# Later loads of token tiles and packed weights, and a lower transfer rate in the plan, in a transformer layer on one core

## The chip, the cores and the metric

The kernel runs on one core of a Trainium2 chip. The metric is device time in microseconds, the median of several executions; smaller is better. The core has five instruction streams that matter here: PE (matrix products; PEld is its loading of weights), DVE, ACT and POOL (elementwise work), and SP, which here only issues DMA transfers. Each stream runs its instructions strictly in the order in which the program lists them and waits wherever an operand isn't ready.

## The reference

One layer with layer norms ahead of its two halves: attention with 32 heads of 32 columns, one shared key and value head, a linear position bias and a causal mask; then one linear map whose weight is packed in six-bit codes. The input is 4 batches of 512 tokens of 1024 columns.

```
q = (LN(x) @ Wq).reshape(b, s, 32, 32)
k, v = split(LN(x) @ Wkv)                       # one head of 32 for all 32 query heads
scores = q k^T / sqrt(32) + slope[h] * (kpos - qpos), masked where kpos > qpos
x = x + (softmax(scores) @ v) @ Wo
codes = 4 six-bit numbers out of each 3 words of qweight     # 1024 x 768 int32 -> 1024 x 1024
x = x + LN(x) @ ((codes - zero_point) * weight_scale)^T + bias
```

## The kernel before

**Work.** Products with Wq and Wo are made of three products each, a high part and a low part of both operands (`hi`, `lo`), to keep precision. The kernel goes through the 4 batches; each batch of 512 tokens has 4 token tiles of 128 (`x_b_t`, loaded by `load_x`, L550), which `layernorm` (L563) normalizes and `chunk` (L591) transposes on PE into eight tiles `xc`. Then come 8 steps for each batch, one for every group of 4 heads, 32 steps in all:

- `queries` (L675): 24 products into the one buffer `pq`; ACT and DVE copy it out as `qh` and `ql` (one buffer each); both are written to DRAM (`q_d`) and read back in another layout as `qs` (three loads) beside the bias rows (`qr_d`).
- `maxima` (L726): products `s` of queries and keys; DVE takes row maxima of them (L751, `junk`); PE turns the maxima (`trm`), and they go as two rows `mt` into `qs` by two small DMAs.
- `attention` (L797): products `st` with those rows in place, exponentials on ACT (`p`), masking and sums of `p` on POOL, products `pav` with the values, and the sums `den`.

After the steps come 16 token tiles (`token_tile`, L995): product with Wo (`po`), layer norm, transposes, product with the unpacked codes (`pf`), and the store.

**Packed weights.** `unpack` (L904) handles an eighth of `qweight`: a load of 393 KB (`qw`, L908), three DVE instructions (`v`), an ACT conversion (`code`), a transposing DMA (`across`, L942), a second ACT conversion (`codes`, L945), and a write of 524 KB to DRAM (`wf_d`). The result is read back only once, by `load_codes` (L952), after the attention steps.

**What sets the order.** The program's order is made on the host by the class `Work`. Every operation is entered with an engine, a cost and a wished time `at` in microseconds. `forward` (L248) runs a model of the five streams: an operation may start when those ahead of it have ended, and not before its `hold`; among the ready ones the earliest wished goes first. In the model a transfer takes `size / DMA_RATE` on one shared DMA resource (L265), plus a fixed latency; with 280.0 that is 1.87 us for 524e3 bytes. `backward` (L285) finds how late each could be, and `order` (L311) repeats both and keeps the order whose modelled end is earliest. In the later passes a transfer is also kept from starting more than `EARLY`, 12 us, ahead of its latest useful time. Before the change only transfers that POOL issues have a `hold`. The model becomes the order in which the instructions stand on each engine; it puts no waiting on the chip beyond the real operands.

**Buffers that matter.** `xc` has 10 tiles: a batch's eight `xc`, and two that `unpack` uses in turn for `qw`, `v` and `codes`. `x` has 4 tiles. `qs` has 3.

The lines at the end of the kernel that set the wished times are these (STEP is 15.0, T0 is 16.0, NG is 8):

```
    for c in range(KC):
        unpack(T0 + (1.6 + 2.0 * (c % 3) + NG * (c // 3)) * STEP, c)
...
        if b:
            for t in range(NT):
                load_x(T - 3.0 * STEP + 3.0 * t, b, t)
            for t in range(NT):
                layernorm(T - 2.0 * STEP + 3.0 * t, b, t)
```

Of the kernel before, what the change touches and what calls it, by code (L numbers as in the profile page):

```python
# [118 lines left out]
class Work:  # L119
# [6 lines left out]
    DMA_LAT = 2000  # L126
    EARLY = 12e3
    TURN = 105
    DMA_RATE = 280.0

    def __init__(self):
        self.ops, self.items = [], []
# [115 lines left out]
    def forward(self, wanted, hold=None):  # L248
# [13 lines left out]
        def done(o, s):  # L262
            if o.size:
                free = s + self.ISSUE[o.eng]
                shared["dma"] = max(shared["dma"], free) + o.size / self.DMA_RATE  # L265
                seen[o.n] = shared["dma"] + self.DMA_LAT
# [18 lines left out]
    def backward(self, start):  # L285
# [7 lines left out]
        def first(o):  # L293
            away = o.size / self.DMA_RATE + self.DMA_LAT if o.size else 0.0
            t = away
            for m in self.edges[o.n]:
                if not o.size:
                    away = self.SAME[o.eng] if self.ops[m].eng == o.eng else o.lat
                t = max(t, until[m] + away)
            return t  # L300
# [36 lines left out]
STEP = 15.0  # L337
# [4 lines left out]
def layer_kernel(  # L342
# [14 lines left out]
    nc = tc.nc  # L357
# [3 lines left out]
    NG = NH // GH  # L361
# [4 lines left out]
    work = Work()  # L366
# [14 lines left out]
    def new(pool_name, tag, shape, dt, name):  # L381

        p, bufs = pools[pool_name]
        return work.item(lambda: p.tile(shape, dt, tag=tag, name=name), (pool_name + tag, bufs))
# [13 lines left out]
    def act(at, n, fn, out, ins, sbuf=False):  # L398
        work.op("ACT", at, n / 1.2 + (90.0 if sbuf else 70.0), fn, out, ins)

    def dve(at, n, fn, out, ins, port=False, more=0.0):
        work.op("DVE", at, n / 0.96 + 75.0 + more, fn, out, ins, port=port)
# [1 line left out]
    def pool_op(at, cost, fn, out, ins):  # L404
        work.op("POOL", at, cost, fn, out, ins, port=True)

    def dma(at, size, fn, out, ins, eng="SP"):
        work.op(eng, at, 0.0, fn, out, ins, size=size)

    def split(at, n, hi, lo, src, hi_it, lo_it, src_it, port=False):  # L410

# [7 lines left out]
    def move(dst, src):  # L419
        return nc.sync.dma_start(out=dst.bitcast(F32), in_=src.bitcast(F32))  # L420
# [22 lines left out]
        out=mask(),  # L443
        in_=mask(),
# [14 lines left out]
    def prep_keys(at, i):  # L459
        dma(  # L460
            at, 61e3, lambda: nc.gpsimd.dma_start(out=kst[i]()[R_BIAS:R_ALL, :], in_=k_rows),
            [(kst[i], "b")], [], eng="POOL",
        )

    def prep_rows(at, g):
        dma(
            at, 229e3, lambda: nc.gpsimd.dma_start(out=qr_d[g], in_=q_rows[g]), [qr_i[g]], [],
            eng="POOL",
        )
# [4 lines left out]
    def prep_wkv(at):  # L474
        st = new("stg", "stg", [P, KC, 2 * HD], F32, "wkv_st")
        src = w_kv.rearrange("(c p) d -> p c d", p=P)
        dma(at, 262e3, lambda: nc.sync.dma_start(out=st(), in_=src), [st], [])
        split(
            at + 18.0, HALF, lambda: wkv()[:, :, 0 : 2 * HD], lambda: wkv()[:, :, 2 * HD :], st,
            (wkv, 0), (wkv, 1), st, port=True,  # L480
        )
# [68 lines left out]
    def load_x(at, b, t):  # L550
        xt = xh[b, t] = new("x", "x", [P, H], F32, f"x_{b}_{t}")
        src = x[b, ts(t, P), :]
        if b or t < NT - 1:
            dma(at, 524e3, lambda: nc.sync.dma_start(out=xt(), in_=src), [xt], [])
            return
        for i in range(2):
            dma(
                at + 0.001 * i, 262e3,
                lambda i=i: nc.sync.dma_start(out=xt()[:, ts(i, HALF)], in_=src[:, ts(i, HALF)]),
                [(xt, i)], [],  # L560
            )
# [342 lines left out]
    def unpack(at, c):  # L904

        qw = new("xc", "xc", [P, H // 4, 3], I32, f"qw_{c}")
        src = qweight[ts(c, P), :].rearrange("p (g w) -> p g w", w=3)
        dma(at, 393e3, lambda: nc.sync.dma_start(out=qw(), in_=src), [qw], [])  # L908
        v = new("xc", "xc", [P, H // 4, 4], I32, f"v_{c}")
        dve(  # L910
            at + 4.0, 256,
            lambda: nc.vector.tensor_scalar(
                v()[:, :, 0:1], qw()[:, :, 0:1], 63, None, ALU.bitwise_and
            ),
            [(v, 0)], [qw], port=True,
        )
        dve(
            at + 4.0, 256,
            lambda: nc.vector.tensor_scalar(
                v()[:, :, 1:2], qw()[:, :, 0:1], 6, 63, ALU.logical_shift_right, ALU.bitwise_and  # L920
            ),
            [(v, 1)], [qw], port=True,
        )
        dve(
            at + 4.0, 256,
            lambda: nc.vector.tensor_scalar(
                v()[:, :, 2:4], qw()[:, :, 1:3], 63, None, ALU.bitwise_and
            ),
            [(v, 2)], [qw], port=True,
        )  # L930
        code = new("stg", "stg", [P, H], BF16, f"code_{c}")
        act(
            at + 5.0, H,
            lambda: nc.scalar.activation(
                code(), v().rearrange("p g j -> p (g j)"), AF.Copy, bias=-CODE_MID
            ),
            [code], [v], sbuf=True,
        )
        across = new("stg", "stg", [P, KC, P], BF16, f"across_{c}")
        dma(  # L940
            at + 6.0, 700e3,
            lambda: nc.sync.dma_start_transpose(out=across(), in_=code()), [across], [code],  # L942
        )
        turned = new("xc", "xc", [P, KC, P], F32R, f"codes_{c}")
        act(at + 12.0, H, lambda: nc.scalar.copy(turned(), across()), [turned], [across], sbuf=True)  # L945
        dma(
            at + 14.0, 600e3,
            lambda: move(wf_d.rearrange("k p n -> p k n")[:, :, ts(c, P)], turned()),
            [(wf_i, c)], [turned],
        )  # L950
# [266 lines left out]
    T0 = 16.0  # L1217
    for t in range(NT):
        load_x(0.01 * t, 0, t)
        layernorm(1.0 + t, 0, t)  # L1220
# [4 lines left out]
        prep_wq(2.0 if g == 0 else T0 + (g - 0.9) * STEP, g)  # L1225
        prep_rows(T0 + g * STEP + (2.0 if g == 0 else -6.0), g)
    for c in range(KC):
        unpack(T0 + (1.6 + 2.0 * (c % 3) + NG * (c // 3)) * STEP, c)
    for b in range(B):
        T = T0 + b * NG * STEP  # L1230
        if b:
# [5 lines that stand above are left out]
            chunk(  # L1237
                T - 4.0 + 0.5 * c if b == 0 else T - 0.9 * STEP + 1.3 * c - 2.6, b, c
            )
        keys_values(T + 6.0 if b == 0 else T - 1.0, b)  # L1240
        for g in range(NG):
            i = b * NG + g
            at = T0 + i * STEP
            queries(at, i)
            maxima(at + 17.0, i)
            attention(at + 34.0, i)
        invert(T + NG * STEP + 48.0, b)
# [52 lines left out]
```

## Time and profile before

| | us |
|---|---|
| median of 3 runs | 826.74 (825.87 to 827.88) |
| the profiled execution | 825.42 |
| its span, first to last instruction | 823.5 |
| PE busy | 795.9 |
| DVE busy | 565.5 |
| POOL busy | 514.1 |
| ACT busy | 372.3 |

The span lies 1.9 us under the profiled execution's time, and that execution 1.3 us under the median. A busy PE is not a PE at its peak: matmuls overlap, and a matmul that is shown with 390 ns is followed by the next after 227 ns where nothing disturbs it. So the busy share of PE says little, and the stretches in which it waits, or in which its clock is low, say more. "PEclk" in the profile is the clock that was granted, as a share of the full one. "DMA share" is the mean busy share of the 16 DMA engines; it passes 1 in places. An entry "[1.45 <-DVE ql L415]" behind an instruction says that its engine stood idle for 1.45 us before it, and that this DVE instruction ended the wait.

### The profile page before, as it was taken

How to read it: one execution, taken by the hardware profiler on the slowest of the kernel's cores; microseconds unless marked ns; L12 is line 12 of the kernel's file. 1: busy time of each engine (PE TensorE's matmuls, PEld its weight loads, DVE VectorE, ACT ScalarE, POOL GpSimd, SP SyncE). 2: the span in 40 equal slices, each digit the busy share in tenths (PEclk: the TensorE clock that was granted, in tenths of full speed). 3: DMA queues.
4: the chain of work that ended last, by engine and by line, in shares of the span. 5: the costliest groups of instructions: out<-in, count | busy, mean ns of one | idle time of the engine just before them, and what ended most of it. 6: DMA issues, size and time to landing. Idle time of an engine off the chain costs nothing.

```text
span 823.5 us, 13425 instructions
## 1 busy us (share of the span) xinstructions
PE 795.9 (97%) x4480; PEld 594.7 (72%) x4480; DVE 565.5 (69%) x1491; ACT 372.3 (45%) x659; POOL 514.1 (62%) x442
## 2 busy tenths in 40 slices
PE   5979999999999999999999999999999999999997
PEld 4756676777676767676775767667888888888885
DVE  7476777388786388777367675644998666666865
ACT  4336575464775445675556564330233323332320
POOL 4337977276787375877489896879465445554333
PEclk9989999999999999999999999999999999999999
DMA  7885853395553387543567966526875755665321
GB/s 223 245 252 154 232 164 91 111 266 188 155 145 100 106 262 211 148 120 111 174 174 194 235 189 208 170 58 171 214 178 158 173 131 129 152 151 137 97 52 51
DMA packets 131796, 133.39 MB, mean 162 GB/s; under 512 B 42964, under 2 KB 93140, under 8 KB 130704
## 3 DMA queue, kind: packets, MB, share of 16 engines
q1 hardware_dynamic: 130912, 129.01, 57.0%
q0 software_dynamic: 816, 3.53, 1.7%
q8 instruction: 35, 0.57, 0.3%
q14 instruction: 33, 0.27, 0.1%
HBM read 85.58 MB, written 39.85 MB: 152 GB/s over the span
## 4 chain that ended last, share of the span: by engine, by line
PE 89%; DVE 4%; DMA 2%; ACT 2%; issue 1%; POOL 1%; SPq 1%; DVEq 0%; ACTq 0%; POOLq 0%
PE po L1047 21%; PE pq L682 21%; PE pf L1167 13%; PE st L819 9%; PE s L738 9%; PE pav L848 8%; PE den L877 4%; PE pkv L616 2%; PE tr L598 2%; DVE junk L751 2%; ACT p L829 1%; POOL p L860 1%; DMA wo_st<-in_L_attn_Wo_dram 1%; DMA qs<-mt 1%; SPq L420 1%
## 5 line engine op out<-in xcount | busy, mean ns | idle before, releaser
L751 DVE CUSTOM_DVE_ANT_0 junk<-s,mask 128x384 f32<-128x384 f32 (+3 forms) x512 | 250.6, 490 | 119.6 <-PE s L738 88.8
L860 POOL TENSOR_TENSOR p<-p,p 128x1536 f32<-128x1536 f32 (+2 forms) x96 | 232.4, 2421 | 16.7 <-PE pav L848 15.0
L829 ACT ACTIVATE p<-st 128x512 f32<-128x512 f32 (+1 forms) x352 | 183.9, 559 | 115.8 <-PE st L819 110.7
L682 PE MATMUL pq<-xc,wqh 128*128 128x512 f32 x512 | 198.5, 405 | 2.3 <-DVE ql L415 1.4
L1047 PE MATMUL po<-woh,aT 128*128 128x512 f32 x512 | 164.8, 391 | 0.0
L838 POOL TENSOR_SCALAR_AFFINE_SELECT p<-p 128x512 f32<-128x512 f32 x128 | 82.2, 647 | 105.1 <-ACT p L829 104.3
L738 PE MATMUL s<-kst,qs 124*128 124x384 f32 (+3 forms) x512 | 127.5, 324 | 3.9 <-DVE mx L751 3.6
L819 PE MATMUL st<-qs,kst 126*128 126x512 f32 (+1 forms) x352 | 127.1, 399 | 3.9 <-ACT p L829 2.9
L1167 PE MATMUL pf<-wf,xT 128*128 128x512 f32 x512 | 121.1, 390 | 0.7 <-DVE xT L415 0.7
L738 PEld LDWEIGHTS s<-kst,qs 124*128 124x128 f32 x512 | 91.5, 189 | 34.2 <-DVE mx L751 8.9
L682 PEld LDWEIGHTS pq<-xc,wqh 128*128 128x128 f32 x512 | 97.7, 191 | 23.8 <-issue 2.7
L1047 PEld LDWEIGHTS po<-woh,aT 128*128 128x128 f32 x512 | 96.1, 188 | 21.7 <-DVE mx L751 0.8
L1167 PEld LDWEIGHTS pf<-wf,xT 128*128 128x128 f32 x512 | 95.8, 188 | 20.9 <-DVE xT L415 1.1
L682 PE MATMUL pq<-xc,wql 128*128 128x512 f32 x256 | 101.8, 398 | 0.1
L1047 PE MATMUL po<-wol,aT 128*128 128x512 f32 x256 | 99.7, 389 | 0.0
L819 PEld LDWEIGHTS st<-qs,kst 126*128 126x128 f32 x352 | 63.5, 190 | 25.7 <-ACT p L829 10.8
L848 PE MATMUL pav<-p,kv 128*32 128x512 f32 (+3 forms) x1024 | 79.9, 436 | 0.0
L848 PEld LDWEIGHTS pav<-p,kv 128*32 128x32 f32 x1024 | 29.6, 109 | 48.8 <-issue 37.6
L1187 POOL TENSOR_TENSOR x<-x,y 128x512 f32<-128x512 f32 x30 | 42.7, 1425 | 27.4 <-DVE y L1178 27.4
L1047 PEld LDWEIGHTS po<-wol,aT 128*128 128x128 f32 x256 | 48.1, 188 | 9.6
L538 POOL TENSOR_SCALAR rstd_f<-mv_f 128x1 f32<-128x1 f32 x16 | 3.9, 244 | 81.7 <-DVE mv_f L533 72.7
L682 PEld LDWEIGHTS pq<-xc,wql 128*128 128x128 f32 x256 | 49.2, 192 | 7.2 <-POOL wql L489 0.6
(92 smaller groups left out, 878.6 us busy)
## 6 DMA issues: line engine op xcount, KB each, us to landing
qs<-q_d SPq DMA_DIRECT2D x96, 256.0 KB
x<-_attn_hidden_states_dram SPq DMA_DIRECT2D x31, 512.0 KB
q_d<-qh SPq DMA_DIRECT2D x32, 256.0 KB
q_d<-ql SPq DMA_DIRECT2D x32, 256.0 KB
at_d<-a SPq DMA_DIRECT2D x32, 256.0 KB
raw<-at_d SPq DMA_DIRECT2D x16, 512.0 KB
raw<-rden_d SPq DMA_DIRECT2D x64, 128.0 KB
out_dram<-x SPq DMA_DIRECT2D x32, 256.0 KB
```

The lines of the kernel that those rows point to most:

```text
L682: nc.tensor.matmul(pq(), w()[:, c, :], xc[b, c]()[:, s, :], start=(c == 0 and n == 0), stop=(c == KC - 1 and n == 2),)
L738: nc.tensor.matmul(ps()[:, o : o + W], q()[0:R_MAX, at, ts(t, P)], k()[0:R_MAX, :W], start=True, stop=True,)
L751: lambda ps=ps, junk=junk, t=t, h=h, W=W, o=o: nc.vector.tensor_tensor_reduce(out=junk()[:, :W], in0=ps()[:, o : o + W], in1=mask()[:, S - ...
L819: nc.tensor.matmul(ps()[:, place, :], k()[0:R_ALL, ts(j, P)], q()[0:R_ALL, mine, j * P :], start=True, stop=True,)
L829: lambda ps=ps, own=own, j=j: nc.scalar.activation(pr[j]()[:, own, :], ps(), AF.Exp),
L838: nc.gpsimd.affine_select(out=d, in_=d, pattern=[[0, GH], [1, P]], compare_op=ALU.is_ge, fill=0.0, base=0, channel_multiplier=-1,)
L848: nc.tensor.matmul(pav()[ts(h, HD), j * P :], kv[b]()[:, j, HD:], pr[j]()[:, h, :], start=(j == 0), stop=(j == NT - 1), tile_position=(0, ...
L860: nc.gpsimd.tensor_tensor(d, d, pr[j](), ALU.add)
L877: nc.tensor.matmul(d()[ts(h, HD), :], onesel()[:, g, :], pr[0]()[:, h, :], start=(g == 0), stop=(g == NG - 1), tile_position=(0, h * HD),)
L1047: nc.tensor.matmul(po(), aT[s][1]()[:, c, :], w()[:, ts(n, HALF)], start=(c == 0 and m == 0), stop=(c == KC - 1 and m == 2),)
L1167: nc.tensor.matmul(pf(), xT()[:, s, c, :], wf[c]()[:, ts(n, HALF)], start=(c == 0 and s == 0), stop=(c == KC - 1 and s == 1),)
L1187: (nc.vector if last else nc.gpsimd).tensor_tensor(d, d, y(), ALU.add)
```

## The change

Four edits. The rate in the model falls from 280 to 240 (bytes per ns). `dma` can set a `hold`. Loads of token tiles of batches 1 to 3 get one, 2.5 steps (37.5 us) ahead of their wished time, and loads of `qw` one 3 us ahead of theirs. And the eight unpackings are wished for one place later: `c + 1` stands where `c` stood.

```
-    DMA_RATE = 280.0
+    DMA_RATE = 240.0
...
-    def dma(at, size, fn, out, ins, eng="SP"):
-        work.op(eng, at, 0.0, fn, out, ins, size=size)
+    def dma(at, size, fn, out, ins, eng="SP", hold=None):
+
+        o = work.op(eng, at, 0.0, fn, out, ins, size=size)
+        if hold is not None:
+            o.hold = hold * 1e3
...
         if b or t < NT - 1:
-            dma(at, 524e3, lambda: nc.sync.dma_start(out=xt(), in_=src), [xt], [])
+            dma(
+                at, 524e3, lambda: nc.sync.dma_start(out=xt(), in_=src), [xt], [],
+                hold=at - 2.5 * STEP if b else None,
+            )
...
-        dma(at, 393e3, lambda: nc.sync.dma_start(out=qw(), in_=src), [qw], [])
+        dma(at, 393e3, lambda: nc.sync.dma_start(out=qw(), in_=src), [qw], [], hold=at - 3.0)
...
-        unpack(T0 + (1.6 + 2.0 * (c % 3) + NG * (c // 3)) * STEP, c)
+        unpack(T0 + (1.6 + 2.0 * ((c + 1) % 3) + NG * ((c + 1) // 3)) * STEP, c)
```

In model time the wished times of the eight unpackings go from 40, 70, 100, 160, 190, 220, 280, 310 us to 70, 100, 160, 190, 220, 280, 310, 340 us. The holds of batch 1's token tiles are at 53.5, 56.5, 59.5 and 62.5 us, those of batch 2 and 3 each 120 us later.

## The prediction

> **What bounds the kernel now.** I read the busy time by stretches first. Columns: the stretch and its length in us; busy us of PE, PEld, DVE, ACT and POOL with counts; the granted PE clock; the DMA share; GB/s.
>
> ```profile
> 16.00:34.00 18.00, 16.49 (x76) 13.33 (x77) 9.59 (x15) 10.10 (x19) 4.94 (x5) 1.00 0.70 177
> 34.00:46.00 12.00, 8.74 (x40) 6.42 (x39) 9.41 (x35) 2.60 (x5) 5.10 (x5) 0.99 1.06 322
> 46.00:63.00 17.00, 14.47 (x49) 10.82 (x50) 12.50 (x45) 7.17 (x10) 6.15 (x12) 0.80 0.78 229
> ...
> 80.00:100.00 20.00, 19.50 (x129) 12.62 (x128) 14.88 (x48) 10.93 (x22) 18.57 (x16) 1.00 0.89 241
> ...
> 120.00:500.00 380.00, 376.16 (x2423) 264.16 (x2425) 266.29 (x921) 216.53 (x416) 267.64 (x214) 1.00 0.58 165
> ...
> 545.00:802.00 257.00, 257.00 (x1163) 210.97 (x1156) 179.67 (x235) 72.35 (x91) 136.69 (x106) 1.00 0.57 142
> ```
>
> PE bounds the kernel nearly everywhere: it doesn't wait at all in 545 to 802, and 3.84 us of the 380 from 120 to 500. Of the 27.6 us in which PE stands idle, 9.1 lie ahead of 16 us and 6.0 behind 802, at the first loads and the last tile. The place where something can be won is 16 to 63: 1.51 + 3.26 + 2.53 = **7.3 us idle**. There the clock falls too; asked for its two low stretches, the same view says 0.50 from 45.84 to 49.26 and from 59.50 to 62.91, with 3.42 and 3.23 us of PE work in them, so about **3.3 us** more. Together 10.6 us.
>
> The second view is PE's timeline there: who ended the waits.
>
> ```profile
> 33.13 0.50 PE L682 MATMUL pq<-xc,wqh 128*128 128x512 f32 x1 [1.45 <-DVE ql L415]
> ...
> 43.05 0.50 PE L738 MATMUL s<-kst,qs 124*128 124x256 f32 x2 [0.91 <-DVE mx L751]
> 45.23 0.27 PE L767 MATMUL trm<-ident,mx 128*16 128x128 f32 x1 [1.68 <-DVE mx L751]
> ...
> 56.55 0.50 PE L738 MATMUL s<-kst,qs 124*128 124x384 f32 x2 [0.55 <-DVE mx L751]
> 57.59 0.50 PE L738 MATMUL s<-kst,qs 124*128 124x384 f32 x2 [0.54 <-DVE mx L751]
> 57.93 0.68 PE L819 MATMUL st<-qs,kst 126*128 126x512 f32 x2
> ```
>
> The waits are for DVE's row maxima. The first step's maxima take DVE from 35.06 to 45.08, the second's from 52.04 to 62.08, and between them DVE has no maxima to take. Until the first `st` at 57.93 PE has nothing to put between them.
>
> The third view, SP's issues, shows why the steps stand so far apart.
>
> ```profile
> 24.79 1.73 SPq L942 DMA_TRANSPOSE across<-code  x1
> 26.63 0.99 SPq L420 DMA_DIRECT2D qs<-q_d  x2
> ...
> 33.86 0.43 SPq L554 DMA_DIRECT2D x<-_attn_hidden_states_dram  x1
> ...
> 35.25 0.98 SPq L554 DMA_DIRECT2D x<-_attn_hidden_states_dram  x2
> 36.73 0.81 SPq L420 DMA_DIRECT2D qs<-q_d  x2
> ...
> 41.36 4.31 SPq L908 DMA_DIRECT2D qw<-in_L_ffn_qweight_dram  x1
> ...
> 46.40 1.70 SPq L420 DMA_DIRECT2D q_d<-qh  x1
> 48.19 0.42 SPq L420 DMA_DIRECT2D q_d<-ql  x1
> 48.70 1.25 SPq L420 DMA_DIRECT2D qs<-mt  x2
> ```
>
> Three token tiles of batch 1 (3 x 524 KB) are issued just ahead of the second step's `qs`, a 524 KB `wf_d` write at 40.50, and a `qw` whose issue takes SP 4.31 us. Behind it stand `qh`, `ql`, and the first step's `mt`, whose high half ACT had ready at 45.80: it leaves 2.9 us late. From the packet records (bytes issued less bytes moved) 1.85 to 2.0 MB are queued at 36.7 to 38.4, and the second step's three `qs` loads have moved their last byte at 42.9, 43.9 and 46.6, 6.2 to 8.2 us after their issue; in the empty queue at 26.6 it took 2.3.
>
> **The change, part by part.**
>
> *Unpackings one place later.* The first now leaves 5 to 60 us and goes to about 67; the other seven move into places that unpackings hold already, and the last ends near 390, far ahead of the first read at 506.9. The first place holds three DVE instructions, 20.11 to 23.58, ahead of `ql` (23.50), though `qh` was done at 22.42: 1.1 us. It holds the `across` issue, 1.73 us of SP, after which the `qs` loads go out at once, and 1.45 us of transfer (26.42 to 27.87) ahead of them; the `wf_d` write; and two ACT conversions of 1.05. So the third `qs` load (issued 28.84), and with it the first `s` at 34.62, comes 1 to 2 us earlier; I take 1.5. The second unpacking's load at 41.36 goes too, with its 4.31 us on SP.
>
> *Token tiles not before 53.5.* Gone from 33.86 to 36.2: 1.57 MB. At 271 GB/s (241 over its share of 0.89) that is 5.8 us of transfer ahead of the second step's `qs`, which would then stand ready before 45, when DVE ends the first maxima. Their layer norms go as well: six DVE statistics of about 0.65 at 41.51 to 48.9, of which the one at 41.51 stands 0.6 us in the first maxima's way. Their first use on PE, the transposes of batch 1, begins at 110.5, so at 53.5 plus some 6 they are not late; what sits on DVE, ACT and POOL for them (1.3, 1.24 and 1.05 us each tile) now falls beside full steps.
>
> *Sum for 16 to 63.* The wait of 1.45 stays: one `pq` buffer. Of the 3.26 us in 34 to 46, 1.2 go: maxima that start earlier without the 0.6, and still set the pace. The 2.53 us in 46 to 63 go: the second maxima follow the first, and `st` has its rows some 5 us sooner. Of the low clock 2.5 of 3.3 go with the idle time in front. **6.2 us less.**
>
> On the low clock: both halvings follow waits of 0.2 to 1.7 us, 2.9 in all from 43.0 to 45.8, then 2.5 from 54.6 to 59.7. The Trainium skill ("TensorE: Matmul & The Clock Gate", Part 1) says that the clock is halved after at least one idle window of some 3.4 us; no single wait here is so long, so the trace shows a stricter gate. By the page's rule the low clock would not have come from these waits, and the 2.5 would be no gain.
>
> *What it adds.* Four token tiles (three new ones) go into 53.5 to 100, where the DMA share is 0.68 (63 to 80) and 0.89, and POOL is busy 18.57 of 20 us. Two unpackings instead of three lie in batch 0, at 67 and 97 instead of 5, 41 and 84. Below, it costs nothing: PE waits 0.5 us in 63 to 120. Above: 5.8 us of transfer, less the 2.2 free in 80 to 100, is 3.6 us of late `qs`, and if PE waits for that, one more low-clock stretch, 1.7: 5.3 us. I take 1.0, nearer to the row that shows hardly a wait at a share of 0.89. The holds put no wait on the chip; but SP's list changes, and an `x` load that now stands ahead of a `qs` or `mt` delays everything behind it.
>
> The Trainium skill ("DMA: Bandwidth & Descriptors", Rules for kernel authors) says to issue a transfer early and wait late, which speaks against the holds. The row at 34 to 46, share 1.06, is the case where early is in someone's way; by the rule alone the token tiles would be better where they are and the 6.2 shrink to what the unpacking gives, about 2.
>
> *Rate 240.* It moves no byte; it makes the model place every reader of a transfer later (524 KB counted as 2.18 us for 1.87). The stretches, GB/s over share, give 177/0.70 = 253, 322/1.06 = 304, 241/0.89 = 271, 142/0.57 = 249, all above 240 and on both sides of 280. What it can win: the waits from 120 to 545, 4.7 us, of which one of 0.81 (323.39) was ended by a DMA, an `mt`. What it can lose: new waits of that kind from another order, six at 0.81 being 5 us. I take 0, between.
>
> **Total:** 6.2 - 1.0 = 5.2 us off the profiled 825.42: 820.2. The median lies 1.3 above that execution: **821.5**.
>
> **Rivals.**
>
> - *The whole hole closes* (0.18). The first steps overlap fully: of the 10.6 us only 1.45 stay, the cost is nothing, and the new order wins 1.5 of the 4.7: 826.7 - 10.6 = 816. For it: DVE is free 49.2 to 52.0, PE has work queued. Against: maxima still need 10 us a step.
> - *Hidden anyway* (0.16). The order on PE stays: `trm` ahead of the fourth `pq`, `st` behind the second `s`; earlier data find no earlier slot, and the gain of 1 to 1.5 is eaten by the 1.0: 826.5.
> - *Slower: collision at 80 to 100* (0.18). The token tiles and their norms land among the Wq loads and `wql` work. Price 5.3, gain in the hole only 1.5 (first `s` earlier): 826.7 + 3.8 = 830.5. It decides if the `x` loads are issued within 80 to 100 ahead of a step's `qs`, and PE's idle time there exceeds the hole's gain.
> - The forecast has 0.48.
>
> **Numbers.** 0.2% (1.7 us) is about what a measurement of this kernel can tell from no change. Faster: forecast 0.48, the whole hole 0.18, a quarter of "hidden" 0.04: 0.70. Same 0.12. Slower 0.18. The range goes from 814.5 (the whole hole, and 1.5 more of the waits behind) to 829.0, which leaves out most of the collision.
>
> **What would show it.** Right: no `qw`, `across` or later-batch `x` issue ahead of 50; a DMA share well under 1 in 34 to 46; the second step's `s` by about 47 instead of 51.60; the first `st` near 50; the clock at 1.00 in most of 46 to 63. Wrong: PE's idle time in 16 to 63 still near 7 (hidden), or over 2 us in 63 to 120 (collision), or over 6 in 120 to 545 (the rate), or any in 545 to 802.

## The result and the profile after

The changed kernel took 835.41 us (831.13 to 838.60, 4 runs) beside 826.61 (825.87 to 827.88, 4 runs) of the kernel before: ratio 1.0094, 95% interval 1.0067 to 1.0121. It is slower by 8.8 us; the forecast was 821.5, faster by 5. The profiled execution is the fastest of the four, 831.13 (span 829.3), so the profile accounts for 5.7 us (831.13 - 825.42), and the other 3 lie in executions that have no profile.

The same stretches of the changed kernel, with the columns of the prediction's first view; the last line but one was not shown of before:

```profile
34.00:46.00 12.00, 10.23 (x43) 7.61 (x42) 9.78 (x36) 2.56 (x5) 3.11 (x4) 0.95 0.71 207
46.00:63.00 17.00, 16.78 (x84) 12.68 (x82) 12.22 (x49) 7.11 (x16) 5.87 (x8) 0.93 0.54 144
...
80.00:100.00 20.00, 16.75 (x95) 9.66 (x94) 16.09 (x54) 15.67 (x29) 12.57 (x16) 1.00 0.68 193
...
500.00:545.00 45.00, 40.59 (x254) 26.41 (x246) 23.65 (x67) 19.29 (x39) 31.90 (x26) 1.00 0.47 143
545.00:802.00 257.00, 254.35 (x1155) 207.59 (x1154) 182.77 (x230) 70.83 (x90) 141.32 (x108) 1.00 0.60 146
```

Before, the stretch from 500 to 545 read

```profile
500.00:545.00 45.00, 44.12 (x277) 31.03 (x273) 25.77 (x64) 20.39 (x41) 31.00 (x26) 1.00 0.55 171
```

The hole at the start has closed: the 49 instructions of PE from 46 to 63 are 84, and its idle time there is 0.22 us instead of 2.53. Two new holes stand against it. In 80 to 100, PE runs 95 instructions for 129 and stands idle 3.25 us; around the end of the attention steps it stands idle 4.41 us (before 0.88) and then 2.65 where it had waited for nothing.

**Lag.** Busy time says little of PE here, since a matmul that waits a little is shown longer (a first `pq` after a wait with 0.50 us, its neighbours with 0.39 to 0.40). So the stages are compared by lag: the time since the span's start, less the work that PE has done by then, each matmul counted by the spacing that it has where nothing disturbs it (0.227 us for 512 columns). Both kernels do the same work, so a stage that adds less lag is a faster one. A few missing records make it uncertain by some tenths.

| lag, us | at 60 | 60 to 120 | 120 to 480 | 480 to 600 | 600 to PE's last product |
|---|---|---|---|---|---|
| before | 25.5 | 6.6 | 30.6 | 6.4 | 0.6 |
| after | 20.6 | 10.8 | 28.1 | 15.6 | 0.7 |
| difference | -4.9 | +4.2 | -2.5 | +9.2 | +0.1 |

The sum, +6.1, is the 5.7 of the two profiled executions within the method's error. The start wins most of what it was meant to win, and the handover from the attention steps to the token tiles, far behind every edited load, takes back nearly twice that.

**The hole at 80 to 100.** PE's timeline in the changed kernel; L688 is `pq`, L744 `s`, L825 `st`:

```profile
82.92 0.63 PE L825 MATMUL st<-qs,kst 126*128 126x512 f32 x2
...
86.18 0.93 PE L825 MATMUL st<-qs,kst 126*128 126x384 f32 x2 [0.73 <-ACT p L835]
...
93.42 0.50 PE L744 MATMUL s<-kst,qs 124*128 124x384 f32 x2 [0.55 <-DVE mx L757]
...
99.16 0.28 PE L773 MATMUL trm<-ident,mx 128*16 128x128 f32 x1 [0.76 <-DVE mx L757]
...
99.76 0.39 PE L688 MATMUL pq<-xc,wqh 128*128 128x512 f32 x1
```

Between 82.9 and 99.8 there is no `pq`: PE has run a whole step's 24 products from 76.5 to 82.9, and from there it goes at the pace of ACT's exponentials and DVE's maxima, with nothing to put between. ACT meanwhile stood idle from 72.56 to 79.01, waiting for a late token tile:

```profile
79.01 1.24 ACT L591 ACTIVATE x<-x,nmr,rstd_a 128x1024 f32<-128x1024 f32 x1 [6.45 <-POOL nmr L584]
```

The tile's load was issued behind 60, not at 34 to 36; its `nmr` stands behind a 3.52 us `p` on POOL. But the tile held up nothing that stands behind it on ACT: done with it, ACT waits another 2.87 us for PE's last `pq` (its `qh` starts at 83.12), and the exponentials of the next step begin at 83.61, when the first `st` at 82.92 has run. So on the chip the place of the 24 `pq`, ahead of that `st`, delays them. Why the model laid the `pq` there, and whether the late tile is the reason, this profile can't say.

**The hole at the handover.** PE's timeline before, over the last `st`, and below it the changed kernel (L1082 and L1088 are `tr`, L1167 `pf`):

```profile
542.07 0.73 PE L1167 MATMUL pf<-wf,xT 128*128 128x512 f32 x2
542.64 0.34 PE L819 MATMUL st<-qs,kst 126*128 126x384 f32 x1
542.82 0.63 PE L1167 MATMUL pf<-wf,xT 128*128 128x512 f32 x2
543.28 0.39 PE L819 MATMUL st<-qs,kst 126*128 126x512 f32 x1
543.52 0.62 PE L1167 MATMUL pf<-wf,xT 128*128 128x512 f32 x2
```

```profile
540.48 0.44 PE L825 MATMUL st<-qs,kst 126*128 126x384 f32 x1 [0.26 <-ACT p L835]
540.85 0.86 PE L854 MATMUL pav<-p,kv 128*32 128x256 f32 x16
541.64 0.62 PE L825 MATMUL st<-qs,kst 126*128 126x384 f32 x2
542.81 0.89 PE L825 MATMUL st<-qs,kst 126*128 126x512 f32 x2 [0.55 <-ACT p L835]
544.05 0.50 PE L825 MATMUL st<-qs,kst 126*128 126x512 f32 x1 [0.36 <-ACT p L835]
```

Before, two `pf` products stand behind nearly every last `st`, and ACT's exponential (0.61 us) runs beside them. After, the `st` stand alone, most wait for ACT, and the 64 `pf` follow in one piece from 548.51. Further on, the `raw` loads of token tile 2 are issued at 546.52 for 531.25, and PE waits 1.25 us at 576.44 for what is made of a later tile.

### The profile page after: what moved, and what is told of

Its sections match the earlier page's. It is cut to its first block, busy times and chain, and to the rows that moved or that the text cites. A ratio compares the mean times of both kernels' runs of the same rounds, so it can differ in the third digit from the quotient of the medians.

```text
span 829.3 us, 13396 instructions
## 1 busy us (share of the span) xinstructions
PE 797.4 (96%) x4480; PEld 593.4 (72%) x4480; DVE 563.9 (68%) x1491; ACT 369.2 (45%) x659; POOL 518.3 (62%) x442
## 4 chain that ended last, share of the span: by engine, by line
PE 82%; DMA 5%; DVE 4%; POOL 4%; ACT 2%; issue 1%; SPq 0%; DVEq 0%; POOLq 0%; ACTq 0%
PE pq L688 20%; PE po L1053 19%; PE pf L1173 11%; PE s L744 8%; PE st L825 8%; PE pav L854 8%; PE den L883 3%; POOL p L866 2%; DMA raw<-rden_d 2%; DVE junk L757 2%; PE pkv L622 2%; PE tr L604 2%; DMA at_d<-a 1%; ACT p L835 1%; POOL raw L1030 1%
## 5 line engine op out<-in xcount | busy, mean ns | idle before, releaser
L688 PE MATMUL pq<-xc,wqh 128*128 128x512 f32 x512 | 197.9, 403 | 2.1 <-DVE ql L418 1.4
L825 PE MATMUL st<-qs,kst 126*128 126x512 f32 (+1 forms) x352 | 128.5, 402 | 6.6 <-ACT p L835 4.4
L744 PE MATMUL s<-kst,qs 124*128 124x384 f32 (+3 forms) x512 | 127.9, 325 | 4.9 <-DVE mx L757 4.5
L744 PEld LDWEIGHTS s<-kst,qs 124*128 124x128 f32 x512 | 90.9, 189 | 37.9 <-DVE mx L757 17.9
L688 PEld LDWEIGHTS pq<-xc,wqh 128*128 128x128 f32 x512 | 97.0, 189 | 22.0 <-DVE ql L418 2.6
L688 PE MATMUL pq<-xc,wql 128*128 128x512 f32 x256 | 101.2, 396 | 0.0
L825 PEld LDWEIGHTS st<-qs,kst 126*128 126x128 f32 x352 | 63.8, 189 | 32.2 <-ACT p L835 18.6
L1151 POOL TENSOR_TENSOR x<-x,rows 128x512 f32<-128x512 f32 x32 | 41.2, 1309 | 32.6 <-DVE x L1074 32.6
L415 ACT CAST aT<-raw 128x1024 fp32r<-128x1024 f32 x16 | 16.8, 1052 | 84.7 <-PE pf L1173 40.6
```

Source lines behind the costliest of these rows:

```text
L688: nc.tensor.matmul(pq(), w()[:, c, :], xc[b, c]()[:, s, :], start=(c == 0 and n == 0), stop=(c == KC - 1 and n == 2),)
L744: nc.tensor.matmul(ps()[:, o : o + W], q()[0:R_MAX, at, ts(t, P)], k()[0:R_MAX, :W], start=True, stop=True,)
L825: nc.tensor.matmul(ps()[:, place, :], k()[0:R_ALL, ts(j, P)], q()[0:R_ALL, mine, j * P :], start=True, stop=True,)
L1151: nc.gpsimd.tensor_tensor(d, d, rows["bias"][n][1](), ALU.add)
```

## The experiments

Each kernel is the changed kernel or the one before with the edit shown. The expectations name theories by letters and say what each expects. Three of them carry the argument to its end. C: what is lost is lost by laying the order anew, whatever the edit. E: the lower rate hurts through the transfers of the first 130 us. F: the loss from 480 to 600 lies in the order of the operations there. Theory A (each edit has its own loss in its own place) and rival B (any new order hits or misses the handover) come first, and D, later, holds the rate to be the cause of the loss, whatever the holds do. Times of the kernel before in the same sessions: 826.8, 827.5, 827.4, 827.6, 827.5.

### One part at a time

Only the rate, on the kernel before:

```
-    DMA_RATE = 280.0
+    DMA_RATE = 240.0
```

> Only the rate in the model is 240; holds and unpackings are as before. Theory A (each loss has its own edit: the late token tiles cost some 5 us in 80 to 100, the rate costs some 8 us where attention hands over to the token tiles, 500 to 600): start as before, idle PE near 7 us in 16 to 63, PE idle some 5 to 7 us in 500 to 600, 832 to 836 us in all. Rival B (each edit lays the whole order anew, and the handover is hit or missed by chance of the order): nothing follows from the rate itself, 824 to 832.

Measured: 839.64 us, ratio 1.0162 (1.0124 to 1.0199). The one edit that moves no load by itself costs more than the whole change, and more than A (832 to 836) or B (824 to 832) gave it.

Only the hold of the token tiles, rate 280 (`hold=at - 2.5 * STEP if b else None` alone added to the kernel before):

> Only the token tiles of batches 1 to 3 are held; rate 280, unpackings as before. Theory A: the start wins 2 to 4 us (second step's queries no longer behind 1.57 MB), PE idles 2 to 4 us in 63 to 100, the handover stays as before (under 1.5 us idle in 500 to 600): 825 to 829. Rival B: the handover can lose 5 us here too: 830 to 834.

Measured: 831.62, ratio 1.0052 (1.0023 to 1.0081).

Only the unpackings (one place later, with the hold of `qw`), rate 280:

```
-        unpack(T0 + (1.6 + 2.0 * (c % 3) + NG * (c // 3)) * STEP, c)
+        unpack(T0 + (1.6 + 2.0 * ((c + 1) % 3) + NG * ((c + 1) // 3)) * STEP, c)
```

> Only the unpackings come one place later, with their hold; rate 280, token tiles early as before. Theory A: the start wins 1.5 to 3 us, no collision in 63 to 100, handover as before: 823 to 825.5. Rival B: 823 to 833, the handover decides.

Measured: 838.21, ratio 1.0144 (1.0095 to 1.0192). Most of it is lost between 120 and 480, where the lag grows by 41.4 us for 30.6; one wait of PE's, ended by DVE's `mt`, takes 4.8 there. No theory had foreseen that (823 to 833).

The whole change without the rate (in the changed kernel `DMA_RATE = 280.0`):

> All of the change but the rate, which stays 280. Theory A: the start as after the change (PE idle near 3.5 us in 16 to 63), the collision in 63 to 100 (near 3.5 us idle), no loss at the handover: 826 to 828. Rival B: handover idle of 4 us or more here too, 830 to 835.

Measured: 830.20, ratio 1.0041 (1.0017 to 1.0064). So 5.2 us (835.41 - 830.20) belong to the rate, and 3.4 stay without it.

The two other pairs, at 240: the changed kernel without the hold of the token tiles (`hold=None`),

> The change without the hold of the token tiles; rate 240, unpackings late. Theory D (the rate is the cause: an order laid out for slow transfers gives PE's time away to cover waits that the chip doesn't have, whatever the holds do): 834 to 841, PE idle 5 us or more in 480 to 600, as in the changed kernel. Rival C (every order is a draw, the rate no worse than another edit): anything from 827 to 841, so that 831 or less speaks for C. Rival A (the tiles are the cause of the collision): 80 to 100 loses under 3 us.

measured 840.54, ratio 1.0172 (1.0148 to 1.0195); and without the later unpackings and their hold,

> The change without the later unpackings and their hold; rate 240, token tiles held. Theory D: 834 to 841, against 831.6 for the same at rate 280. Rival C: 827 to 841, and 831 or less speaks for C.

measured 836.85, ratio 1.0119 (1.0101 to 1.0136).

With these six and both kernels each edit has four pairs that differ in it alone. **The rate** costs +12.9 alone, +5.2 with the tiles' hold, +2.3 with the unpackings, +5.2 with both: mean +6.4. The tiles' hold gives +4.9, -8.0, -2.8 and -5.1: mean -2.8. The unpackings give +11.4, -1.4, +0.9 and -1.4: mean +2.4. The rate is the only part with one sign in all four, though its 2.3 is not clear of noise (1.0172 beside 1.0144, with intervals that overlap). Theory D's ranges held for no_tiles and no_unpack (834 to 841). The parts don't add up (12.9 + 4.9 + 11.4 alone, 8.8 together).

### Is it the laying anew?

The kernel before with all wished times behind T0 moved by 50 ns, which changes nothing but the order that the model lays:

```
-    T0 = 16.0
+    T0 = 16.05
```

> The kernel before with T0 at 16.05 for 16.0: every wished time past the start 0.05 us later, an edit that means nothing. Theory C (the loss is not what the edits mean: any edit lays all 4,390 operations anew, and the order before is an unusually good draw, which any redraw loses, above all in 60 to 120 and at the handover, 500 to 600): slower than before by 3 to 12 us, 830 to 838. Rival A (each loss has its own edit): within 1.5 us of before, 825 to 828.

Measured: 828.49 (826.47 to 837.16), ratio 1.0033 (0.9981 to 1.0084). The total hardly moves, but the stages do: the lag at 60 is 21.9 for 25.5, and 480 to 600 adds 11.9 for 6.4. Its last two stretches, beside which before has 118.94 us of PE work in the last:

```profile
120.00:480.00 360.00, 357.90 (x2289) 251.97 (x2281) 246.84 (x871) 200.74 (x389) 247.37 (x198) 1.00 0.58 162
480.00:600.00 120.00, 115.71 (x643) 83.53 (x642) 73.34 (x147) 39.40 (x73) 92.41 (x70) 1.00 0.59 170
```

So theory C holds for the handover: it goes bad without any of the edits. It fails for the total (830 to 838 expected) and for 60 to 120, where this order adds 6.0 of lag for 6.6, and it doesn't explain the rate's 12.9.

### Keeping parts of the old order

These kernels don't let the model lay the order; they list it:

```
-    ordered = work.order()
+    ordered = [work.ops[n] for n in ORDER]
```

First, the order of before with only the changed operations moved: loads and norms of token tiles as late as the hold has them, each unpacking in the next one's place.

> The meaning of the change without a new order: the order before, as a list, in which only the loads and norms of the token tiles of batches 1 to 3 stand no earlier than their holds, and each unpacking stands in the next one's place. Theory C: the start wins 2 to 5 us and the rest keeps what it had, 822 to 825. Rival A with my price for the collision: the late tiles cost 3 to 5 us in 60 to 100 here too, 826 to 831.

Measured: 838.80, ratio 1.0142 (1.0124 to 1.0159). Second, the changed kernel's order up to 60 us, and that one behind it:

> The order after the change for what it places ahead of 60 us of model time, and behind it the order of moved_in_old_order. Theory C: the 4.9 us that the changed kernel is ahead at 60 us are kept in good part, 822 to 824.5. Rival A: the tiles that come late collide with the Wq loads, the lead is gone by 100 us, 826 to 830.

Measured: 841.94, ratio 1.0170 (1.0142 to 1.0198). Both are worse than the change, and than anything that was expected of them. PE's longest group of waits in the first:

```profile
PE st L822 <- ACT p L832: 8.4, 10, 3.4
```

An operation that is moved alone takes its wait for late data with it and holds up what stands behind it on its engine. One of these ten waits shows it: ACT stands idle for 2.64 us until 75.63 for a moved tile's `nmr`, starts the next exponentials only at 77.24, and at 77.89 a wait of PE's for them ends, 1.99 us long. That the others come about in the same way is likely, not shown. The Trainium skill ("PSUM — Partial Sum Buffer", Engine vs sequencer instructions) says that ScalarE, VectorE and GpSimd take their queues strictly first in, first out; these waits are in keeping with it. So these two say nothing of the gain at the start.

Third, the changed kernel's order for what before places ahead of 440 us, and the order of before behind:

> The order after the change for all that the order before places ahead of 440 us of model time, and the order before for the rest. Theory C (the handover is lost by the order of the operations there): 500 to 600 costs as before, not 8 us more, the 2 us lead at 440 stays, 822 to 827. Rival (the handover is lost by what comes earlier, or by the transfers' state): 500 to 600 still costs 6 us more or so, 830 to 836.

Measured: 831.92, ratio 1.0062 (1.0041 to 1.0084). The stretch from 480 to 600 is mended (7.4 of lag for 15.6), but 13.8 are added in 400 to 480, at the seam, with one wait of 4.20 for POOL's `p` at 462 (the changed kernel adds 5.2 in that stretch). The likely reason is that this seam cuts through steps whose data are not yet made; seams at 386, 398, 404 and 492, below, cost no such wait.

### How much of a rate, how much of a hold

The whole change with `DMA_RATE = 270.0`:

> The whole change with a rate of 270 in place of 240. Theory D: most of the loss is gone, 825 to 830. Rival C: as likely 830 to 838 as less. My predicted gain of the holds and unpackings alone, without any loss behind: 821.5.

Measured: 827.52, ratio 1.0004 (0.9988 to 1.0020), as D expected (825 to 830). The whole change at 280 with the token tiles held 3.0 steps ahead of their wished time, 7.5 us less of a delay:

```
-                hold=at - 2.5 * STEP if b else None,
+                hold=at - 3.0 * STEP if b else None,
```

> The whole change at rate 280, and the token tiles held until 3.0 steps ahead of their wished time, not 2.5 (46 us in place of 53.5 for the first). Theory D: near the kernel before, 824 to 829. Rival C: 827 to 838. Rival A (late tiles collide): a us or two better than the 830.2 of 2.5 steps.

Measured: 830.40, ratio 1.0040 (1.0022 to 1.0059). From 60 to 120 it adds 6.7 of lag, as before does, for 9.6 with the hold of 2.5 steps at the same rate; what it wins there it loses from 480 to 600 (13.8).

### Where the rate hurts

In the changed kernel, 240 only for transfers that the model has wished ahead of 130 us (the same in `backward`):

```
-                shared["dma"] = max(shared["dma"], free) + o.size / self.DMA_RATE
+                shared["dma"] = max(shared["dma"], free) + o.size / (240.0 if o.at < 130.0 else 280.0)
```

> The whole change, but the model counts 240 for transfers that it places ahead of 130 us and 280 for the later. Theory E (the rate does its harm where the model's transfers are thickest, 60 to 120): that stage costs over 10 us against PE's pure work, as with 240 throughout (mean 14.8), and the kernel takes 833 to 839. Rival (the rate harms everywhere, or by chance): 60 to 120 near 8, 828 to 832.

Measured: 833.22, ratio 1.0078 (1.0054 to 1.0101). And the reverse, 280 ahead of 130 us and 240 behind:

> The whole change, with 280 for transfers that the model places ahead of 130 us and 240 for the later. Theory E: 60 to 120 costs 6 to 10, as with 280, the handover 9 to 14 as any new order, 828 to 832. Rival (the rate's loss is at the handover): 834 to 839.

Measured: 842.00, ratio 1.0186 (1.0161 to 1.0211). The first of the two lies in E's range (833 to 839), the second refutes it (828 to 832): with the early transfers at 280, the kernel is the slowest of all that the model laid, and it loses early. So theory E is wrong. PE's timeline there has one wait that is longer than all of before's from 60 to 545 together (5.2):

```profile
83.30 0.80 PE L743 MATMUL s<-kst,qs 124*128 124x384 f32 x2 [6.50 <-DVE mx L756]
```

The order is chosen as a whole by its modelled end, so a rate for late transfers changes the early order too. Why it then prefers such an early order is open.

### The handover by itself

Two splices with their seams elsewhere. The order of the rate 270 kernel ahead of 492 us of its own model time, that of before behind:

> The order of the whole change with rate 270 for what it places ahead of 492 us of model time; behind that the order before. Theory F (the handover's loss is the order of its own operations, and the old order happens to have a good one): 480 to 600 costs 6 to 7.5 us against PE's pure work, not 9.5, and the kernel takes 823 to 826. Rival (it comes from what is done earlier, or how far the queries run ahead): 9 to 12 there, 827 to 830.

Measured: 826.00, ratio 0.9988 (0.9975 to 1.0001); 480 to 600 adds 8.4 for 9.5, more than the 6 to 7.5 that F gave it. The order of the 50 ns kernel ahead of 386 us, that of before behind:

> The order of the kernel before with T0 at 16.05, ahead of 386 us of model time; behind that the order before. Theory F: the lead of 4 us that null_shift has at 480 is kept, 480 to 600 costs 6 to 7.5, not 11.9: 821 to 824. Rival: the handover costs 10 or more, 827 to 830.

Measured: 825.88, ratio 0.9975 (0.9956 to 0.9994); 7.3 for 11.9. The handover is as F expected, the time (821 to 824) is not: the lead at the start is gone (lag 24.9 at 60 for 21.9). Then the test on the change itself, its order for all that before places ahead of 398 us, that of before behind:

```
ORDER = sorted(..., key: (0, start_after[n]) if start_before[n] < 398 else (1, start_before[n]))
```

> The order after the change for what the order before places ahead of 398 us of model time, the order before for the rest. Theory F: 480 to 600 costs 6 to 8.5 us against PE's pure work, not 15.6, the seam under 3 us: 826 to 830 against 835.4. Rival (the loss is carried in from earlier): 10 or more there, 832 to 836.

Measured: 825.87 (824.05 to 830.80, 10 runs), ratio 0.9987 (0.9969 to 1.0006). Nothing of the change's loads, holds or rate is undone ahead of 398; only the order behind is the old one, and 9.5 us are gone from 835.41. PE over the last `st` (L822) has the `pf` (L1170) between them again:

```profile
542.48 0.34 PE L822 MATMUL st<-qs,kst 126*128 126x384 f32 x1
542.66 0.62 PE L1170 MATMUL pf<-wf,xT 128*128 128x512 f32 x2
543.12 0.40 PE L822 MATMUL st<-qs,kst 126*128 126x512 f32 x1
543.35 0.63 PE L1170 MATMUL pf<-wf,xT 128*128 128x512 f32 x2
```

Theory F holds for the handover. Last, the same splice at 404 with the order of the 3.0 steps kernel, which had the least lag from 60 to 120 of the orders with the change's holds:

> The order of hold_3 for what the order before places ahead of 404 us of model time, the order before for the rest. Theory F: the handover falls from 13.8 to 6 to 8.5, 823 to 826 against 830.4. Rival: 828 to 832.

Measured: 823.34 (821.87 to 823.92, 4 runs), ratio 0.9940 (0.9918 to 0.9962). It beats both kernels. Its stretches:

```profile
60.00:120.00 60.00, 58.85 (x376) 40.63 (x378) 40.93 (x150) 39.32 (x76) 49.22 (x46) 1.00 0.72 197
...
480.00:600.00 120.00, 118.84 (x672) 87.81 (x672) 75.00 (x157) 39.60 (x72) 91.23 (x70) 1.00 0.60 172
```

PE idles 1.16 us from 480 to 600, for 1.06 before. In lag the profiled execution keeps 2.3 of the start's gain and gives 0.8 back behind 60; it is the second longest of the four (823.85), so the other 2.5 of the 4.1 us are not seen in a profile. It is also the best of several orders that were tried, and graft_null, which has none of the edits, gains too (0.9975). How much of the 4.1 is due to the edits, and how much to a good draw among orders, is not shown.

### All beside each other

Lag in us of the profiled execution, and the median time. "Laid for" is the rate by which the model laid the order.

| kernel | laid for | median | at 60 | 60 to 120 | 120 to 480 | 480 to 600 |
|---|---|---|---|---|---|---|
| before | 280 | 826.7 | 25.5 | 6.6 | 30.6 | 6.4 |
| null_shift | 280 | 828.5 | 21.9 | 6.0 | 30.3 | 11.9 |
| tiles_only | 280 | 831.6 | 24.5 | 9.6 | 29.0 | 12.8 |
| unpack_only | 280 | 838.2 | 22.2 | 10.3 | 41.4 | 12.1 |
| no_rate | 280 | 830.2 | 25.1 | 9.6 | 29.3 | 13.4 |
| hold_3 | 280 | 830.4 | 23.7 | 6.7 | 28.8 | 13.8 |
| rate_270 | 270 | 827.5 | 23.1 | 10.2 | 26.8 | 9.5 |
| after | 240 | 835.4 | 20.6 | 10.8 | 28.1 | 15.6 |
| rate_only | 240 | 839.6 | 26.0 | 15.2 | 27.9 | 13.8 |
| no_tiles | 240 | 840.5 | 20.0 | 17.1 | 36.3 | 10.4 |
| no_unpack | 240 | 836.9 | 25.3 | 16.0 | 28.7 | 8.3 |
| early_240 | both | 833.2 | 19.3 | 10.7 | 35.8 | 10.6 |
| late_240 | both | 842.0 | 21.1 | 15.1 | 32.7 | 15.6 |
| graft_270 | spliced | 826.0 | 22.7 | 10.7 | 27.4 | 8.4 |
| graft_null | spliced | 825.9 | 24.9 | 6.6 | 31.3 | 7.3 |
| graft_after | spliced | 825.9 | 19.5 | 11.9 | 30.8 | 6.7 |
| graft_hold3 | spliced | 823.3 | 23.2 | 6.9 | 30.8 | 6.7 |

Two columns carry the reading. From 60 to 120, the six orders laid for 240 in whole or in part add 14.2 on average, the seven for 270 or 280 add 8.4: that is where most of the rate's cost shows. In the change itself its 5.2 can't be placed: there the stretch adds 10.8 for no_rate's 9.6, and the two profiles can't be set beside each other, being of the fastest of four executions (831.13) and of the slowest of ten (833.86). From 480 to 600 every newly laid order adds 8.3 to 15.6, whatever its rate, and the order of before 6.4 to 8.4 in before and the four splices; in moved_in_old_order and new_start_60, which have it with operations moved, some 8 and 9. So the two groups touch.

## Why the prediction was wrong, step by step

*Sum for 16 to 63 (6.2 us less): near in total, its reasons right only in part.* Lag at 60 is 4.9 less. Of idle time 3.9 went (1.5 in 34 to 46, 2.3 in 46 to 63) for a forecast of 3.7; of the two low-clock stretches one stayed (from 44.9, 3.41 us), so about 1.6 went for 2.5. The second step's `s` begins at 47.32 for a forecast of 47, the first `st` at 53.54 for 50, and no `qw`, `across` or later token tile is issued ahead of 60. The DMA share of 34 to 46 fell from 1.06 to 0.71. The size shifts with the clock: the 50 ns kernel and its splice have the same order up to 386 us, and 21.9 and 24.9 at 60. The gain goes with the unpackings. PE idles from 16 to 63 for 7.30 us before and 3.44 after; with the tiles' hold but the old unpackings it is 5.56 (tiles_only) and 7.61 (no_unpack), though no token tile of batch 1 is issued there ahead of 48; with later unpackings and no hold it is 3.81 (unpack_only) and 4.11 (no_tiles). In these two the model laid the tiles' loads later by itself (from 47.97 and 57.89), so the hold was not needed for it. Nor were the bytes what kept the second step's `s` back:

```profile
51.60 0.63 PE L738 MATMUL s<-kst,qs 124*128 124x512 f32 x2
```

This is PE's timeline before. The `s` has no wait ahead of it, 5 us after the 46.6 at which its last `qs` had moved; it stood that far behind in PE's order. So the gain came with another order; what the bytes out of the way gave by themselves is not shown.

*What it adds (1.0): mis-sized.* From 60 to 120 the lag grows by 4.2 more than before, inside the bounds (0 to 5.3) but at the other end. The choice was "nearer to the row that shows hardly a wait at a share of 0.89"; the DMA share of 80 to 100 is in fact lower than before (0.68), and still PE idles 3.25 us there, while in 63 to 80, at a share of 0.98, it idles 0.42. The share was the wrong measure: what is missing there is `pq` for PE to run beside the maxima and exponentials, not room for bytes. With half a step less of hold the price from 60 to 120 is 0.1 instead of 3.0 (6.7 and 9.6 for 6.6, both at 280), by one pair of orders.

*Rate 240 (0): the step that failed.* "I take 0, between" weighed only PE's waits for transfers. The rate costs 6.4 on average over four pairs (2.3 to 12.9) and 5.2 in this change, and no new waits for transfers account for it: PE's waits in the changed kernel, the longest groups behind the first load,

```profile
PE s L744 <- DVE mx L757: 4.5, 12, 0.6
PE st L825 <- ACT p L835: 4.4, 11, 0.7
PE st L825 <- DMA qs<-mt: 1.8, 1, 1.8
```

have one DMA among them (at 506.70, where an `mt` shares the time with three `wf` loads of 524 KB issued from 501.24). In rate_only, with its 12.9, the profile names no wait of PE's that a DMA ended. The rate's cost is that of another order. Of the rates tried with all the rest of the change, 270 did best (827.5, beside 830.2 at 280 and 835.4 at 240).

*The handover (no term in the sum): the other step that failed.* The first view read "it doesn't wait at all in 545 to 802", and the prediction priced the places that the edits touch. But the edits go through a planner that lays all 800 us anew, and the order of before happened to be a good one at the handover. This is the largest term, +9.2 in the profiled execution, and graft_after shows that it goes with the order of the operations behind 398 (15.6 becomes 6.7), with the change's own order ahead of it. The rate's 5.2 is the loss split by edit and the handover's 9.2 the loss split by stage; they overlap and can't be added. Which of the differences there decides (no `pf` between the last `st`, the `raw` load 15 us later, the `wf` loads around the `mt`) was not taken apart.

*The rivals.* The collision came nearest by its total, 830.5, and had the place (80 to 100) and nearly the price (5.3 for 4.2), but not its mechanism: it wanted the `x` loads issued within 80 to 100, and they were issued from 60.2 to 64.6. And it held the start's gain down to 1.5, which was 4.9. The signals named for a wrong forecast fired: 3.67 us idle in 63 to 120 (bound 2), 7.2 in 120 to 545 (bound 6), and 2.65 in 545 to 802 (none allowed).

*What stays open.* Why a rate that only later transfers are planned by spoils the order of 60 to 120; in which stage the change pays the rate's 5.2; and the 4 us by which the median of the changed kernel lies over its profiled execution.

## What to carry to other kernels

An edit to a planner's input is an edit to the whole schedule: lay the same plan anew with an edit that means nothing, see which stages move, and put that spread into the range before pricing the edit itself. When a stage is won and a far one lost, keep the old order behind a seam at which the data of both orders are ready; that turned a loss of 8.8 us into no difference (ratio 0.9987, 0.9969 to 1.0006), and with a shorter delay at the old rate into a gain of 4.1, of which a part may be a lucky draw. And read the room for moved work by what stands behind it in the engines' queues, not by the share of the DMA engines that is free.

## What the runs showed of the chip

The half clock came without a long wait. In the changed kernel it was granted at 0.50 for 3.41 us from 44.9, after three waits of 0.54, 0.54 and 0.55 that ended at 42.04, 43.08 and 44.12; the splice with the same order there (graft_after) had the same three, ended at 42.39, 43.43 and 44.48, and a clock of 1.00 from 16 to 60. Of the four kernels with this order at the start, the other two (new_start_60 and old_end_440) had a low stretch too. The 50 ns kernel had waits of 1.68 and 1.34 us at 45.46 and 47.07 and no low clock; its splice, with 1.68 and 2.19 in the same places, had 6.83 us of it. PE's work and clock there:

```profile
16.00:60.00 44.00, 38.06 (x173) 30.04 (x174) 29.24 (x89) 19.72 (x37) 16.14 (x17) 1.00 0.88 244
```

```profile
16.00:60.00 44.00, 37.12 (x158) 28.89 (x158) 26.27 (x76) 17.91 (x33) 14.94 (x15) 0.92 0.85 226
```

The first is the 50 ns kernel, the second its splice: the same operations in the same order, and 15 instructions of PE fewer by 60 us. The Trainium skill ("TensorE: Matmul & The Clock Gate", Part 1) says that the gate's window runs free of the kernel, so that the place of a change varies from run to run, which is in keeping with this; that it takes an idle window of some 3.4 us does not agree with waits of 0.5 us. A gain that is read from low-clock stretches of one profile, as the 2.5 us of the prediction were, can thus come or go with the execution.
